# Which rounds the exp of a block's last two VectorE chunks stands in

## The chip, the cores and the metric

The kernel runs on one core of one Trainium2 chip. Its time is the device time of one execution in microseconds (us), the median of three runs. TensorE (PE) multiplies matrices, VectorE (DVE), ScalarE (ACT) and GpSimd (POOL) work on tiles, and SyncE (SP) issues DMAs. Each engine runs its own instructions in the order in which the program holds them; they meet through semaphores.

## What is computed

There are two layers over a graph of N = 3327 nodes with D = 128 features. Layer 0 is an attention whose score is a sum of a row's and a column's number, with a residual and a layer norm. Layer 1 is the long one:

```python
q = (x @ Wq.T).reshape(d, n, h)      # d = 128 maps, n = 3327, h = 8
k = (x @ Wk.T).reshape(d, n, h)
v = (x @ Wv.T).reshape(d, n, h)
a = jnp.einsum('dnh,dmh->dnm', q, k) * d ** -0.5
a = a + adj + adj                    # spatial and edge encoding are both adj
a = jax.nn.softmax(a, axis=2)
out = jnp.einsum('dnm,dmh->dnh', a, v).reshape(n, h * d) @ Wo.T
x = layernorm(x + out)
```

So there are 128 attention maps of 3327 x 3327, each of inner size 8, and every one of their 1.4 billion scores needs an exp.

## The kernel before

**Tiling.** The 128 maps are taken in NG = 32 groups of HG = 4 (variable `g`). The 3327 queries are cut into NBLK = 7 blocks (`b`), six of 476 columns and one of 472 that counts; the 3327 keys into NT = 26 chunks (`i`) of 128 or 127 partitions. A **block** of the program is one pair (g, b): 4 maps x 476 queries against all 26 chunks. There are 32 x 7 = 224 blocks, one after the other, and the engines go from one into the next without a barrier.

**One chunk.** TensorE makes the scores (L154) in two halves of two maps each, 128 x 952 a half, into PSUM tiles `scb`. There are then two ways to exp(2(score + adj)). For the chunks in `times` (i = 0, 3, ..., 24; nine of them) ScalarE takes the exp of a half straight out of PSUM (L1136) and GpSimd multiplies it by exp(2 adj) (L1137). For the other 17, the **VectorE chunks**, VectorE adds adj to the scores of a half and writes the sum `e4` to SBUF (L1139), and ScalarE takes the exp there, in place (L968, in `exp_late`). At last TensorE multiplies each chunk's `e4` by the values and sums over the chunks in `av` (L938, in `products`), which VectorE copies out once a block (L948).

**Rounds.** The order is written out by hand (`rounds`, L917 to L927). The chunks stand in stretches of three, (0, 1, 2), (3, 4, 5), ..., (21, 22, 23), and a last one of two, (24, 25). A stretch (i, i+1, i+2) has three rounds: [(i, 1), (i+1, 0)], [(i, 0), (i+1, 1)], [(i+2, 0), (i+2, 1)], where (i, h) is half h of chunk i. The last stretch has the first two alone. So a block has NR = 26 rounds, called R0 to R25 here, each with two halves; R24 is [(24, 1), (25, 0)] and R25 is [(24, 0), (25, 1)]. R0 of the next block follows R25.

In a round the program issues, in this order: the scores of its two halves (four matmuls, L1125); a few units of side work on TensorE (`work_tensor`); for each half the direct exp and multiply, or the add; then `exp_late(now)`, that is, the exps that earlier rounds have put down in the list `late` for this round; the products of the chunk that stands LAG = 4 rounds back in `order`; and side work on VectorE and GpSimd (`work`). Side work is layer 0 of later rows and the output of earlier ones. Function `lane` gives it room for one VectorE unit in every third round from R4, and in R0, R24 and R25; for one TensorE unit in R3, in every third round from R4, and in R24 and R25.

**The list `late`** (L1142 to L1150) says in which round a VectorE chunk's exp is issued. Its general rule is the last branch: the whole chunk, 128 x 1904, one round after its second half was added. Two chunks of a block have a branch of their own, because 26 % 3 is 2. Chunk 25 (`NT - 1`) has its exp in two halves, each two rounds after its add, so they stand in R0 and R1 of the next block. Chunk 23 (`NT - 3`), whose two adds are both in R23, has its exp in two halves, in R24 and in R25.

**Buffers.** `scb` of the `times` chunks has one PSUM buffer (pool `pe`), so the scores of the next direct exp are computed only after the one before has been read; those of the VectorE chunks have two (pool `pd`). `e4` has seven.

## Time and profile before

| | |
|---|---|
| median of 3 runs (lowest to highest) | 10004.5 us (10001.76 to 10006.51) |
| profiled execution: time, span | 10004.91 us, 10003.1 us |
| ACT busy | 9892.4 us, 99% of the span |
| PE busy | 9461.4 us, 95% |
| DVE busy | 9334.1 us, 93% |
| POOL busy | 9201.7 us, 92% |
| granted TensorE clock | 0.996 |
| L968 ACT exp in SBUF | 4256 instructions, 7104.0 us |
| L1136 ACT exp out of PSUM | 4032 instructions, 4078.6 us |
| L1139 DVE add | 7616 instructions, 8420.0 us |

Read it so: busy time is the time that lies under an engine's instructions, and ScalarE's and VectorE's instructions overlap their neighbours a little, so the sum of the durations (7104.0 + 4078.6 us for ScalarE) is more than the busy time, and even more than the span. In a run of back-to-back instructions what one of them takes is the distance from the end of the one before to its own end, not its duration. The page's 40 slices show the same shares from the second to the last but one: the 224 blocks are alike.

The timeline shows instructions of one engine by start (us from the span's start), duration and line; equal neighbours are merged (x2, x3), and what the engine waited for stands in brackets.

### The profile page before, as it was taken

What the parts mean: (1) busy time and instruction counts of PE and PEld (TensorE: products, weight loads), DVE (VectorE), ACT (ScalarE), POOL (GpSimd) and SP (SyncE); (2) the same over time, 40 slices, a digit from 0 to 9 for tenths busy, and PEclk for the clock granted to TensorE, in tenths of its full rate; (3) what the DMA queues carried; (4) which work ended last, traced back from release to release, by engine and by line L of the source; (5) the groups of instructions that cost most, each with busy time, mean ns of one, the idle gap of its engine ahead of it and who ended that gap; (6) DMA issues with size and microseconds to landing.
All of it is one profiled execution on the core that took longest, in us unless ns stands there. A gap on an engine that the chain in (4) does not pass through costs nothing.

```text
span 10003.1 us, 212173 instructions
## 1 busy us (share of the span) xinstructions
PE 9461.4 (95%) x81923; PEld 3078.5 (31%) x81923; DVE 9334.1 (93%) x11592; ACT 9892.4 (99%) x8352; POOL 9201.7 (92%) x4416
## 2 busy tenths in 40 slices
PE   7999999999999999999999999999999999999998
PEld 2233333333233333323333332333332333332222
DVE  7999999999999999999999999999999999999998
ACT  7999999999999999999999999999999999999998
POOL 7999999999999999999999999999999999999998
PEclk9999999999999999999999999999999999999999
DMA  7665666655656656656566665566665566656554
GB/s 200 200 176 169 177 172 177 178 167 174 177 165 175 182 161 178 177 169 176 165 173 174 181 179 164 163 178 179 177 174 168 164 179 177 175 161 171 167 168 125
DMA packets 1383200, 1728.31 MB, mean 173 GB/s; under 512 B 347463, under 2 KB 1370657, under 8 KB 1378079
## 3 DMA queue, kind: packets, MB, share of 16 engines
q1 hardware_dynamic: 1371828, 1712.03, 60.1%
q8 instruction: 644, 10.55, 0.4%
q10 hardware_dynamic: 10347, 2.61, 0.1%
q14 instruction: 381, 3.12, 0.1%
HBM read 1610.23 MB, written 103.93 MB: 171 GB/s over the span
## 4 chain that ended last, share of the span: by engine, by line
ACT 40%; PE 24%; POOL 16%; issue 11%; DVE 6%; DMA 2%; SPq 1%; POOLq 0%; ACTq 0%; DVEq 0%
ACT e L968 25%; POOL e L1137 16%; ACT e L1136 15%; PE scb L154 12%; PE av L938 11%; DVE e L1139 4%; PE bank L243 1%; DVE o L948 1%; DVE lo L408 0%; DMA q4b<-qT 0%; POOL w L319 0%; DMA at<-ftd 0%; DVE hi L405 0%; DMA k4b<-kT 0%; DVE w L310 0%
## 5 line engine op out<-in xcount | busy, mean ns | idle before, releaser
L1137 POOL TENSOR_TENSOR e<-e,at 128x952 f32<-128x952 f32 (+1 forms) x4032 | 8956.7, 2237 | 718.9 <-ACT e L1136 641.7
L1139 DVE TENSOR_TENSOR e<-scb,at 128x952 f32<-128x952 f32 (+1 forms) x7616 | 8420.0, 1143 | 579.3 <-PE scb L154 477.8
L968 ACT ACTIVATE e<-e 128x1904 f32<-128x1904 f32 (+2 forms) x4256 | 7104.0, 1678 | 2.0 <-DVE e L1139 1.6
L938 PE MATMUL av<-e,v4b 128*32 128x476 f32 x46592 | 5917.6, 572 | 60.6 <-DVE o L948 41.9
L154 PE MATMUL scb<-q4b,k4b 32*128 32x476 f32 (+1 forms) x23296 | 3749.2, 486 | 442.8 <-ACT e L1136 370.8
L1136 ACT ACTIVATE e<-scb 128x952 f32<-128x952 f32 (+1 forms) x4032 | 4078.6, 1012 | 57.5 <-PE scb L154 33.8
L154 PEld LDWEIGHTS scb<-q4b,k4b 32*128 32x128 f32 (+1 forms) x23296 | 1764.2, 189 | 5371.8 <-ACT e L1136 3489.9
L938 PEld LDWEIGHTS av<-e,v4b 128*32 128x32 f32 x46592 | 1059.2, 108 | 1140.0 <-issue 933.0
L243 PE MATMUL bank<-hsb,w 128*32 128x129 f32 (+1 forms) x5200 | 277.8, 285 | 0.0
L328 DVE TENSOR_SCALAR_CACHE_REDUCE dump<-a 128x384 bf16<-128x384 f32 (+2 forms) x468 | 247.1, 528 | 0.6
L319 POOL TENSOR_TENSOR w<-w,a 128x384 f32<-128x384 f32 (+3 forms) x225 | 207.7, 923 | 0.1
L310 DVE TENSOR_SCALAR w<-trow,er 128x129 f32<-128x129 f32 x650 | 201.1, 338 | 0.0
L948 DVE COPY o<-av 128x476 f32<-128x476 f32 (+1 forms) x224 | 145.9, 651 | 8.1 <-PE av L938 7.2
L243 PEld LDWEIGHTS bank<-hsb,w 128*32 128x32 f32 (+1 forms) x5200 | 102.4, 108 | 148.0 <-issue 148.0
L408 DVE SCALAR_TENSOR_TENSOR lo<-bank,hi 128x128 fp32r<-128x128 f32 (+1 forms) x400 | 116.5, 291 | 13.8
L405 DVE TENSOR_SCALAR hi<-bank 128x128 fp32r<-128x128 f32 (+1 forms) x400 | 112.0, 280 | 0.0
L243 PE MATMUL bank<-wv,x1T 128*32 128x128 f32 x1600 | 85.6, 286 | 3.9 <-DVE vb L429 3.9
L243 PE MATMUL bank<-wq,x1T 128*32 128x128 f32 x1600 | 85.4, 285 | 0.0
L243 PE MATMUL bank<-wk,x1T 128*32 128x128 f32 x1600 | 85.4, 285 | 0.0
L243 PE MATMUL bank<-wo,ot 128*32 128x128 f32 x1600 | 85.2, 285 | 0.0
L429 DVE COPY vb<-bank 128x128 f32<-128x128 f32 (+1 forms) x200 | 56.1, 281 | 5.8 <-PE bank L243 5.8
L503 PE MATMUL bank<-ident,o 128*128 128x128 f32 x225 | 52.0, 304 | 0.0
(123 smaller groups left out, 659.7 us busy)
## 6 DMA issues: line engine op xcount, KB each, us to landing
at<-in_adjT_dram SPq DMA_DIRECT2D x1536, 476.0 KB
at<-ftd SPq DMA_DIRECT2D x1674, 238.0 KB
at<-in_adjT_dram SPq DMA_DIRECT2D x256, 472.0 KB
at<-ftd SPq DMA_DIRECT2D x279, 236.0 KB
k4b<-kT SPq DMA_DIRECT2D x128, 415.9 KB
q4b<-qT SPq DMA_DIRECT2D x1528, 29.8 KB
at<-in_adjT_dram SPq DMA_DIRECT2D x186, 208.2 KB
a<-in_adjT_dram SPq DMA_DIRECT2D x50, 504.0 KB
```

What stands on the lines that cost most here:

```text
L154: nc.tensor.matmul(dst, k4[32 * j : 32 * j + H4, first_key(i) : first_key(i) + 2 * r - 1 : 2], q4[32 * j : 32 * j + H4, :nb], start=True, ...
L243: nc.tensor.matmul(dst[c0:c1], w[:, c0:c1], mov, **kw)
L310: nc.vector.tensor_scalar(w, s["t"][:, :, :T3], e, None, op0=ALU.max)
L319: nc.gpsimd.tensor_tensor(w, w, s["a"][n][:, c0 - i0 : c1 - i0, :r], op=ALU.mult)
L328: nc.vector.tensor_scalar(z, a, float(k), None, op0=ALU.is_equal, op1=ALU.add, accum_out=even[:, t, at : at + 1])
L408: nc.vector.scalar_tensor_tensor(lo[:r, o : o + QW], s["b"][:r, :QW], scale, hi[:r, o : o + QW].bitcast(F32), op0=ALU.mult, op1=ALU.subtract,)
L938: nc.tensor.matmul(s.av[32 * j : 32 * j + 32, : s.w], s.v4[:r, j, i * H1 : i * H1 + 32], e[:r, j, : s.w], start=(s.left == NT - 1), stop=( ...
L948: nc.vector.tensor_copy(o4[:, :w], s.av[:, :w])
L968: nc.scalar.activation(e, e, AF.Exp, scale=2.0)
L1136: nc.scalar.activation(eh, z[:r, :, :w], AF.Exp, scale=2.0)
L1137: nc.gpsimd.tensor_tensor(eh, eh, ah, op=ALU.mult)
L1139: nc.vector.tensor_tensor(eh, z[:r, :, :w], ah, op=ALU.add)
```

## The change

```diff
                             if i in times:
                                 continue
                             if NT % 3 == 2 and i == NT - 1:
-                                late.append((now + 2, s, i, 2 * h, 2 * h + 2))
-                            elif NT % 3 == 2 and i == NT - 3:
-                                late.append((now + 1 + h, s, i, 2 * h, 2 * h + 2))
+                                late.append((now + 1, s, i, 2 * h, 2 * h + 2))
                             elif added[i] == 2 and (now + 1, s, i, 0, HG) not in late:
                                 late.append((now + 1, s, i, 0, HG))
```

Chunk 25 keeps its exp in two halves, but each is issued one round after its add: half 0 in R25, half 1 in R0 of the next block. Chunk 23 falls under the general rule: one whole exp, in R24. Nothing else is edited. ScalarE's order from R24 on, with D for a direct exp, h for a late half and W for a whole, and the chunk in brackets:

| round | before | after |
|---|---|---|
| R24 | D(24) h(23) | D(24) W(23) |
| R25 | D(24) h(23) | D(24) h(25) |
| R0 | D(0) h(25) | D(0) h(25) |
| R1 | D(0) h(25) | D(0) |
| R2 | W(1) | W(1) |
| R3 | D(3) W(2) | D(3) W(2) |

The order on TensorE, VectorE, GpSimd and the DMA queues is unchanged.

## The prediction

> **What bounds the kernel now.** I read the busy shares first, then what ScalarE waits for, then one passage from a block to the next, engine by engine. The first line of the page:

> ```profile
> PE 9461.4 (95%) x81923; PEld 3078.5 (31%) x81923; DVE 9334.1 (93%) x11592; ACT 9892.4 (99%) x8352; POOL 9201.7 (92%) x4416
> ```

> ScalarE is full, and what it lacks of the span lies mostly ahead of its first exp at 66 us. The view of the line of the late exps says what it waits for there:

> ```profile
> its engine sat idle before it (us, times) until:
>   DVE e L1139: 1.6, 4
> ```

> 4256 late exps lost 1.6 us in all to VectorE's adds. So today the adds are always early enough; how early decides this case. Now the passage from one block to the next, ScalarE's timeline from R24 on:

> ```profile
> 5075.51 1.06 ACT L968 ACTIVATE e<-e 128x952 f32<-128x952 f32 x1
> 5076.40 1.02 ACT L1136 ACTIVATE e<-scb 128x952 f32<-128x952 f32 x1
> 5077.24 1.07 ACT L968 ACTIVATE e<-e 128x952 f32<-128x952 f32 x1
> 5078.13 1.03 ACT L1136 ACTIVATE e<-scb 128x952 f32<-128x952 f32 x1
> 5078.99 1.05 ACT L968 ACTIVATE e<-e 127x952 f32<-127x952 f32 x1
> 5079.88 1.02 ACT L1136 ACTIVATE e<-scb 128x952 f32<-128x952 f32 x1
> 5080.72 2.74 ACT L968 ACTIVATE e<-e 127x952 f32<-127x952 f32 x2
> 5083.36 0.96 ACT L1136 ACTIVATE e<-scb 128x952 f32<-128x952 f32 x1
> 5084.22 1.78 ACT L968 ACTIVATE e<-e 128x1904 f32<-128x1904 f32 x1
> ```

> These are h(23), D25 (the direct exp of R25), h(23), D0 (that of R0), h(25), D1, then h(25) and W(1) merged, D3, W(2). The ends stand at 5076.57, 5077.42, 5078.31, 5079.16, 5080.04, 5080.90, 5083.46, 5084.32, 5086.00: no gap anywhere. From end to end a late half takes 0.89, a direct half 0.85, a whole 1.68; read the same way in 190 blocks, the medians are 0.886, 0.854 and 1.680. As a check, 15 wholes, 4 late halves and 18 direct ones make 44.12 us, and the median block takes 44.11. So ScalarE's ends are the clock of the kernel.

> **What the change removes.** One late exp a block: chunk 23's two halves become one whole. End to end that is 2 x 0.886 - 1.680 = **0.092 us**, x 224 blocks = 20.6 us. The mean durations say something else:

> ```profile
> L968 ACT ACTIVATE e<-e 128x1904 f32<-128x1904 f32 x2880 | 5299.5, 1840 | 1.0 <-DVE e L1139 0.9
> ...
> L968 ACT ACTIVATE e<-e 128x952 f32<-128x952 f32 x384 | 425.0, 1107 | 0.0
> ```

> 2 x 1.107 - 1.840 = 0.374 us would be 84 us, but neighbours overlap, so a duration is not what an instruction takes. [...]

> **What it moves.** Each of four exps comes at least a round or half a round earlier.
> - W(23) in R24 needs both adds of R23. Its slot is that of the h(23) at 5075.51; the second add ends at 5075.05 in this block. Over 222 blocks the add ends 0.40 us ahead of the slot (median; 0.33 in the tenth percentile). The smallest distance from an add's end to the whole exp that needs it is 0.093 us, met over a dozen times in the trace, so I take 0.09 for the handover. Nothing is lost here; in the few blocks below that it costs under 0.1.
> - The halves of 25 keep about 2 us to their adds. Nothing.
> - D25 comes 0.79 us later behind D24 (a whole between them for a half). D25, h, D0, h, D1 then follow each other as before, and so do TensorE and VectorE, whose scores for R0 and R1 wait for D25 and D0 to read the one `scb` buffer: they only idle 0.8 us more in R25.
> - **W(1) now follows D1 at once**; the h(25) that stood between is gone. W(1) needs the add of (1, 1), and this is the point of the case.

> VectorE's and TensorE's timelines of the same passage (in TensorE's, L154 are scores, L938 products):

> ```profile
> 5079.79 1.15 DVE L1139 TENSOR_TENSOR e<-scb,at 128x952 f32<-128x952 f32 x1
> 5081.18 3.36 DVE L1139 TENSOR_TENSOR e<-scb,at 128x952 f32<-128x952 f32 x3 [0.24 <-PE scb L154]
> 5084.48 0.65 DVE L948 COPY o<-av 128x476 f32<-128x476 f32 x1
> 5085.05 1.14 DVE L1139 TENSOR_TENSOR e<-scb,at 128x952 f32<-128x952 f32 x1
> 5086.11 0.54 DVE L328 TENSOR_SCALAR_CACHE_REDUCE dump<-a 128x384 bf16<-128x384 f32 x1
> ...
> 5086.73 2.21 DVE L1139 TENSOR_TENSOR e<-scb,at 128x952 f32<-128x952 f32 x2
> ```

> ```profile
> 5079.21 0.50 PE L154 MATMUL scb<-q4b,k4b 32*128 32x476 f32 x4 [0.21 <-ACT e L1136]
> ...
> 5081.41 1.42 PE L938 MATMUL av<-e,v4b 127*32 127x476 f32 x8
> ```

> The chain: D0 ends 5079.16, scores 5079.21 to 5079.71, add (1, 1) 5079.79 to 5080.94. It hangs on D0 alone and can't be earlier. **First wait:** W(1) can start at 5080.94 + 0.09 = 5081.03 and, with the 1.78 of an exp that had to wait, ends 5082.81; back to back it would end 1.68 after D1, at 5082.58. Lost: 0.23. In R0 a side unit stands between VectorE's two adds; where it is long, the wait is longer. Block by block in the trace the mean is **0.27**.

> **Then VectorE runs behind.** It does (2, 0), (2, 1), (4, 0), copy, (4, 1), a side unit, (5, 0), (5, 1) nearly without a gap, and ScalarE now comes 0.89 - 0.23 = 0.66 earlier to each. In this block: W(2) needs 5083.39 + 0.09, its slot is 5083.56: nothing. W(4) needs (4, 1), whose end stays between 5086.09 and 5086.19 (0.1 of (4, 0)'s place was TensorE's products of chunk 25, 1.42 instead of 1.00 because they waited for h(25); that wait goes). W(4) then ends at 5087.96 to 5088.06 instead of 5087.87: 0.09 to 0.19 lost. W(5) needs (5, 1), today 5087.79 to 5088.94; it may come up to 0.2 earlier, since ahead of (5, 0) VectorE waited for scores that waited for D3, and D3 is earlier now. Lost: 0.13 to 0.22 here, nothing where R4's side unit is short. From R6 on VectorE's slack of a stretch exceeds what is left.

> The sum over a block is bounded from both sides. If VectorE kept today's distance to D0 throughout, the largest shortfall is 0.65 us (mean of 222 blocks). With every gap after (2, 0) taken out it is 0.37. I take **0.45**: 0.27 + 0.09 + about 0.09, nearer the lower end, because TensorE's two waits do go. 223 passages x 0.45 = 100.4 us.

> **Sum.** 10003.1 - 20.6 + 100.4 = 10082.9 us of span; the profiled execution's time is 1.8 over its span: 10084.7. The median of the runs is 0.4 below the profiled time: **10084**.

> Costed at nothing: GpSimd's multiplies (2.24 each) of the four direct exps R24 to R1, which now come 2.53, 1.74, 1.74 apart instead of thrice 1.74. The products that need the last of them stand in R5, over 3 us later; if that cover went, the products would wait as they do in 79 places today, 38 us in all. DMAs and side work keep their places.

> **Rivals.**
> - *Only the first wait*: VectorE catches up in R2 to R4, the rest of the slack suffices. For it: 0.24 of idle ahead of (2, 0). Against: that idle is TensorE's and stays. 223 x 0.27 - 20.6 = +40: 10044. Chance 0.16.
> - *No catching up*: VectorE's gaps stay though D3 is early. 223 x 0.65 - 20.6 = +124: 10129, or more if the lag reaches the next stretches. Chance 0.16.
> - *Hidden (the other side)*: the add of (1, 1) comes early enough because VectorE and TensorE had 0.8 us more ahead of R0, and the whole exp's 20.6 us remain: 9984. It decides where the loss a block falls under 0.092, that is, where the add ends 0.14 earlier behind D0 than it does. Against it: the scores start 0.05 after D0's end, so time won before D0 isn't passed on. Chance 0.06.
> - *Balance*: a loss of 0 to 0.18 a block, around 10010. Chance 0.08.
> - The forecast, 10050 to 10120: 0.54.

> **Range and chances.** 10032 (the first wait at its least, 0.22: 49 - 21 = +28) to 10135. About 0.2% (20 us) is what a measurement of this kernel tells from no change: faster 0.06, same 0.09, slower 0.85.

> **What would show it.** L968 has 4032 instructions, its 128x952 form gone. The idle time ahead of L968 put down to VectorE's add goes from 1.6 us to about 50 to 100. W(1) starts 0.09 after the add of (1, 1) in nearly every block, and W(4), W(5) in many. VectorE idles 0.8 longer ahead of the add of (1, 0). Wrong if W(1) starts back to back behind D1, if the add of (1, 1) ends less than 2.7 us after D0's start (today 2.81 in the median), or if the lost time lies at a direct exp (a score that is late) rather than at a late one.

## The result and the profile after

The changed kernel takes **10121.3 us** (median of 4 runs, 10116.48 to 10122.84) beside 10003.13 us (9998.15 to 10006.51) of the kernel before in the same session: ratio **1.0117**, 95% interval 1.0105 to 1.013. The forecast was 10084, range 10032 to 10135: right side, inside the range, 37 us short.

The first line of the page of the profiled execution (span 10118.8 us):

```profile
PE 9385.6 (93%) x81923; PEld 3053.3 (30%) x81923; DVE 9293.8 (92%) x11592; ACT 9933.1 (98%) x8128; POOL 9210.5 (91%) x4416
```

224 instructions fewer on ScalarE (8352 to 8128), and every engine's share is lower: all of them wait more. The same passage from a block to the next as in the prediction, first ScalarE: D0, h(25), D1, W(1), D3, W(2):

```profile
5135.37 1.03 ACT L1136 ACTIVATE e<-scb 128x952 f32<-128x952 f32 x1
5136.23 1.06 ACT L968 ACTIVATE e<-e 127x952 f32<-127x952 f32 x1
5137.12 1.02 ACT L1136 ACTIVATE e<-scb 128x952 f32<-128x952 f32 x1
5138.27 1.79 ACT L968 ACTIVATE e<-e 128x1904 f32<-128x1904 f32 x1
5140.18 0.97 ACT L1136 ACTIVATE e<-scb 128x952 f32<-128x952 f32 x1
5141.04 1.78 ACT L968 ACTIVATE e<-e 128x1904 f32<-128x1904 f32 x1
```

Read the ends again: D1 5138.14, W(1) 5140.06, D3 5141.15, W(2) 5142.82. The steps are 1.92, 1.09, 1.67, where back to back they are 1.68, 0.85, 1.68. So 0.24 are lost at W(1) and another 0.24 at D3. Over 190 blocks of full width the median steps are 1.927, 1.079 and 1.679, and 0.904 at D6 instead of 0.854: lost 0.25, 0.23, 0 and 0.05, together 0.53.

VectorE and TensorE in that passage:

```profile
5135.44 1.15 DVE L1139 TENSOR_TENSOR e<-scb,at 128x952 f32<-128x952 f32 x1 [1.06 <-ACT e L1136]
...
5137.03 1.15 DVE L1139 TENSOR_TENSOR e<-scb,at 128x952 f32<-128x952 f32 x1
5138.42 3.26 DVE L1139 TENSOR_TENSOR e<-scb,at 128x952 f32<-128x952 f32 x3 [0.24 <-PE scb L154]
5141.60 0.64 DVE L948 COPY o<-av 128x476 f32<-128x476 f32 x1
```

```profile
5134.71 0.60 PE L154 MATMUL scb<-q4b,k4b 32*128 32x476 f32 x4 [0.88 <-ACT e L1136]
...
5138.65 1.01 PE L938 MATMUL av<-e,v4b 127*32 127x476 f32 x8
5139.59 0.53 PE L154 MATMUL scb<-q4b,k4b 32*128 32x476 f32 x4
...
5142.30 1.00 PE L938 MATMUL av<-e,v4b 128*32 128x476 f32 x8 [0.24 <-DVE o L948]
```

Three readings. The add of (1, 1) ends at 5138.18 and W(1) starts at 5138.27, the handover of 0.09. D3 starts at 5140.18, 0.06 after its scores (5139.59 to 5140.12), which stand in TensorE's queue behind the products of chunk 25. And TensorE idles 0.88, VectorE 1.06 us in R25, for D25: that idling is new.

The waits listed for the late exps' line:

```profile
its engine sat idle before it (us, times) until:
  DVE e L1139: 13.6, 45
```

Only 13.6 us (1.6 before; the prediction named 50 to 100 as a sign), though the wait at W(1) costs a quarter of a microsecond in each of 223 passages. The view counts the gap between a recorded end and the next start. Back to back the next exp starts some 0.18 before the end of the one ahead, and a wait first eats that overlap: of the 0.24 lost at W(1) above, 0.13 is left as a gap. The 45 gaps that are listed are all over 0.15 us, so most of the 223 are not among them. Here only end-to-end steps show what a wait costs.

### The profile page after: what moved, and what is told of

It is laid out like the page before. It is cut to its first block, busy times and chain, and to the rows that moved or that the text cites. A ratio compares the mean times of both kernels' runs of the same rounds, so it can differ in the third digit from the quotient of the medians.

```text
span 10118.8 us, 212173 instructions
## 1 busy us (share of the span) xinstructions
PE 9385.6 (93%) x81923; PEld 3053.3 (30%) x81923; DVE 9293.8 (92%) x11592; ACT 9933.1 (98%) x8128; POOL 9210.5 (91%) x4416
## 4 chain that ended last, share of the span: by engine, by line
ACT 43%; PE 19%; POOL 16%; issue 11%; DVE 8%; DMA 3%; SPq 1%; ACTq 0%; POOLq 0%; DVEq 0%
ACT e L968 30%; POOL e L1137 16%; ACT e L1136 13%; PE scb L154 9%; PE av L938 9%; DVE e L1139 6%; DVE o L948 1%; DMA at<-in_adjT_dram 1%; DMA k4b<-kT 1%; DMA q4b<-qT 1%; DVE lo L408 0%; DVE hi L405 0%; DVE w L310 0%; PE bank L243 0%; SPq L734 0%
## 5 line engine op out<-in xcount | busy, mean ns | idle before, releaser
L1139 DVE TENSOR_TENSOR e<-scb,at 128x952 f32<-128x952 f32 (+1 forms) x7616 | 8385.7, 1143 | 736.2 <-PE scb L154 486.5
L968 ACT ACTIVATE e<-e 128x1904 f32<-128x1904 f32 (+3 forms) x4032 | 7019.0, 1741 | 38.2 <-DVE e L1139 13.6
L938 PE MATMUL av<-e,v4b 128*32 128x476 f32 x46592 | 5852.5, 574 | 112.1 <-DVE o L948 93.1
L154 PE MATMUL scb<-q4b,k4b 32*128 32x476 f32 (+1 forms) x23296 | 3752.8, 487 | 580.9 <-ACT e L1136 531.2
L1136 ACT ACTIVATE e<-scb 128x952 f32<-128x952 f32 (+1 forms) x4032 | 4030.9, 1000 | 94.8 <-PE scb L154 40.5
L154 PEld LDWEIGHTS scb<-q4b,k4b 32*128 32x128 f32 (+1 forms) x23296 | 1767.2, 189 | 5509.3 <-ACT e L1136 3462.1
L938 PEld LDWEIGHTS av<-e,v4b 128*32 128x32 f32 x46592 | 1031.6, 108 | 1141.5 <-issue 880.7
L328 DVE TENSOR_SCALAR_CACHE_REDUCE dump<-a 128x384 bf16<-128x384 f32 (+2 forms) x468 | 247.3, 528 | 0.6
L948 DVE COPY o<-av 128x476 f32<-128x476 f32 (+1 forms) x224 | 144.1, 644 | 5.5 <-PE av L938 5.5
```

The lines of the kernel that those rows point to most:

```text
L154: nc.tensor.matmul(dst, k4[32 * j : 32 * j + H4, first_key(i) : first_key(i) + 2 * r - 1 : 2], q4[32 * j : 32 * j + H4, :nb], start=True, ...
L328: nc.vector.tensor_scalar(z, a, float(k), None, op0=ALU.is_equal, op1=ALU.add, accum_out=even[:, t, at : at + 1])
L938: nc.tensor.matmul(s.av[32 * j : 32 * j + 32, : s.w], s.v4[:r, j, i * H1 : i * H1 + 32], e[:r, j, : s.w], start=(s.left == NT - 1), stop=( ...
L948: nc.vector.tensor_copy(o4[:, :w], s.av[:, :w])
L968: nc.scalar.activation(e, e, AF.Exp, scale=2.0)
L1136: nc.scalar.activation(eh, z[:r, :, :w], AF.Exp, scale=2.0)
```

## The experiments

Theory A, as it stood after this comparison: ScalarE lost 0.53 us a block by waits that begin at D0, less 0.09 for the instruction saved. The rival, B in most runs: another part of the change, or another engine, is to blame. All ratios are against the kernel before, run on the same chip. "D0 to D6" is the distance between the starts of the direct exps of R0 and R6, the median over the trace's full-width blocks; it is 10.29 us in the kernel before and 9.93 in the changed one, where ScalarE back to back would need 9.40.

**Chunk 23's whole exp alone** (chunk 25 as before):

```diff
-                            elif NT % 3 == 2 and i == NT - 3:
-                                late.append((now + 1 + h, s, i, 2 * h, 2 * h + 2))
```

> Chunk 23's whole exp alone; chunk 25 keeps its halves two rounds after their adds. ScalarE: D24 W(23) D25, D0 h(25) D1 h(25) W(1): nothing stands between D25 and D0. Theory A (a direct exp behind another waits for its scores, because the one scb buffer is read by the first; a late exp between them hides that): D0 starts about 0.62 us after D25's end (0.05 to the scores, 0.5 for the four matmuls, 0.06 on), where it would start 0.17 before it; with 0.96 of a direct exp that had to wait its end comes 0.72 late. No wait at W(1) or D3, since h(25) is back between D1 and W(1). 0.72 - 0.09 = 0.63 a block, x 223 = +140: about 10143. Theory B (the loss of the changed kernel belongs to chunk 25's move alone, and the whole exp is free): 20 us faster than before, 9983.

Measured: 10171.88 us, ratio 1.0163 (1.0148 to 1.0179). D25 and D0 in one block, then TensorE's scores of R0 between them:

```profile
5159.11 1.02 ACT L1136 ACTIVATE e<-scb 128x952 f32<-128x952 f32 x1
5160.84 0.96 ACT L1136 ACTIVATE e<-scb 128x952 f32<-128x952 f32 x1 [0.70 <-PE scb L154]
```

```profile
5160.18 0.59 PE L154 MATMUL scb<-q4b,k4b 32*128 32x476 f32 x4 [0.89 <-ACT e L1136]
```

Two direct exps in a row cost 0.82 us (end to end 1.67 instead of 0.85): more than my 0.72, since the four matmuls took 0.59 where I had taken 0.5. Theory B falls: the whole exp isn't free where it leaves a direct exp without a late one behind it. TensorE idles for D25 as long as in the changed kernel (0.89 and 0.88 us), but behind D0 nothing is lost here: the median steps at W(1) and D3 are 1.681 and 0.853, and D0 to D6 is 10.22.

**Chunk 25's halves early, alone** (chunk 23 in halves as before):

```diff
-                                late.append((now + 2, s, i, 2 * h, 2 * h + 2))
+                                late.append((now + 1, s, i, 2 * h, 2 * h + 2))
```

> Chunk 25's halves one round after their adds, as in the changed kernel; chunk 23 keeps its two halves. ScalarE: D24 h(23) D25 h(23) h(25) D0 h(25) D1 W(1). Theory A (the loss comes from W(1) following D1 at once): the waits of the changed kernel at W(1) (0.28 a block) and at D3 (0.27) are there in full, and the 20.6 us of the removed half are not won: the changed kernel's 10121 plus 21, about 10140. Theory B (the loss comes from the whole exp of 23, which puts D25 0.79 later and the three direct exps D25, D0, D1 close together): no loss, about 10004.

Measured: 10167.12 us, 1.0156 (1.0141 to 1.0172). The waits are the changed kernel's: steps of 1.926 and 1.081 at W(1) and D3, D0 to D6 9.96, the median block 44.62 us. (44.62 - 44.11) x 223 = 114 us of the 161, so theory B (no loss) falls. The other 47 us I had not expected. In 41 blocks, each 1.1 to 1.3 us longer (one 1.5), TensorE's granted clock drops. Stretches of the trace (start and end, length, busy time and instructions of PE, its weight loads, DVE, ACT and POOL, then the granted clock, DMA share and GB/s):

```profile
852.00:856.00 4.00, 2.60 (x24) 0.67 (x19) 3.27 (x7) 4.00 (x6) 4.00 (x3) 1.00 0.59 183
856.00:860.00 4.00, 4.00 (x24) 0.65 (x20) 2.37 (x3) 3.28 (x3) 4.00 (x3) 0.57 0.58 186
860.00:864.00 4.00, 3.55 (x40) 1.24 (x36) 3.96 (x6) 3.31 (x3) 3.44 (x2) 1.00 0.04 9
```

A stretch in which TensorE is busy 2.60 of 4 us is followed by one at a clock of 0.57, that is, 3.4 us at 0.50. One matmul of the products takes 1.00 us in such stretches of this run and 0.56 outside them (medians), which is why the blocks that hold one are longer. Past the first 730 us and ahead of the last blocks there is no such drop in the kernel before, and there are 14 in the changed one. The blocks that hold them are 14 us longer in sum, 12% of its loss. Each part of the change alone costs more than the two together (166 and 161 us against 118).

**The other way round**: chunk 23 in halves as before, chunk 25's exp whole by the general rule:

```diff
-                            if NT % 3 == 2 and i == NT - 1:
-                                late.append((now + 2, s, i, 2 * h, 2 * h + 2))
-                            elif NT % 3 == 2 and i == NT - 3:
+                            if NT % 3 == 2 and i == NT - 3:
                                 late.append((now + 1 + h, s, i, 2 * h, 2 * h + 2))
```

> The other way round: chunk 23 in two halves as before, chunk 25's exp whole, one round after its second add (R0). ScalarE: D24 h(23) D25 h(23) D0 W(25) D1 W(1) D3 W(2): as many instructions as in the changed kernel, and again one late exp behind each direct one. Theory A (only the distance from D0 to W(1) and D3 matters): from D0's start to W(1) there are 0.86 + 1.68 + 0.85 = 3.39 us; the add of (1, 1) ends 2.81 after D0's start, so no wait, and D3's scores, ready 3.8 us after D0's start plus 1.03 of D0, meet a D3 at 5.07. The 0.092 a block is won: 20 us faster than before, about 9983. Theory B (VectorE has no slack around the block's end, so that any exp taken out there is lost again in waits): within 10 us of before.

Measured: **9982.91 us**, 0.9978 (0.9969 to 0.9988): faster than both kernels, with the changed kernel's number of instructions. D0, W(25), D1, W(1), D3:

```profile
5065.39 1.03 ACT L1136 ACTIVATE e<-scb 128x952 f32<-128x952 f32 x1
5066.25 1.84 ACT L968 ACTIVATE e<-e 127x1904 f32<-127x1904 f32 x1
5067.93 1.01 ACT L1136 ACTIVATE e<-scb 128x952 f32<-128x952 f32 x1
5068.77 1.85 ACT L968 ACTIVATE e<-e 128x1904 f32<-128x1904 f32 x1
5070.46 1.02 ACT L1136 ACTIVATE e<-scb 128x952 f32<-128x952 f32 x1
```

The ends, 5068.09, 5068.94, 5070.62, 5071.48 from W(25) on, are 0.85, 1.68, 0.86 apart: no wait. The median block takes 44.00 us (44.11 before), D0 to D6 is 10.11, over the 9.93 that the other engines need. So the 0.092 us of the saved instruction are real, and it is the place of the whole exp that decides: between D0 and D1 it gives the others 0.8 us behind D0; between D24 and D25 it takes them away, and ScalarE's own 9.40 is under the 9.93.

**The changed kernel without the products of chunk 25:**

```diff
-                for j in range(HG):
+                for j in range(HG if i < NT - 1 else 0):
                     nc.tensor.matmul(
```

> The changed kernel without the products of chunk 25 (eight matmuls, about 0.95 us of TensorE in R2, between the scores of R2 and those of R3); that part of the sum over keys is left out of the output. Theory A (D3's wait of 0.27 is TensorE's queue: the scores of R3 stand behind those products): D3's wait goes; the wait at W(1) stays at 0.28; with D3 in time, W(4) and W(5) meet VectorE's adds and lose some 0.1 to 0.2 together, as the prediction had it. 10121 - 60 + 20 to 45: 10080 to 10105. Theory B (all of the loss is VectorE's lag, and D3's wait only one place where it shows): no change, 10121.

Measured: 10155.89 us, 1.0142 (1.0126 to 1.0157), *slower* than the changed kernel. From W(1) on: W(1), D3, W(2), D4, W(4), D6:

```profile
5152.67 1.79 ACT L968 ACTIVATE e<-e 128x1904 f32<-128x1904 f32 x1
5154.36 0.95 ACT L1136 ACTIVATE e<-scb 128x952 f32<-128x952 f32 x1
5155.21 1.78 ACT L968 ACTIVATE e<-e 128x1904 f32<-128x1904 f32 x1
5156.89 0.95 ACT L1136 ACTIVATE e<-scb 128x952 f32<-128x952 f32 x1
5157.79 1.79 ACT L968 ACTIVATE e<-e 128x1904 f32<-128x1904 f32 x1
5159.69 0.97 ACT L1136 ACTIVATE e<-scb 128x952 f32<-128x952 f32 x1
```

And VectorE's copy of `av`, with the first products of the new block, which wait for it:

```profile
5156.00 0.64 DVE L948 COPY o<-av 128x476 f32<-128x476 f32 x1
```

```profile
5156.69 1.01 PE L938 MATMUL av<-e,v4b 128*32 128x476 f32 x8 [0.24 <-DVE o L948]
```

D3's wait is gone, its end 0.85 behind W(1)'s. But W(4) and D6 now wait, and D0 to D6 is 9.93 to the hundredth; the median block, 44.54, is the changed kernel's. So D3's wait was one place where a longer delay showed, as theory B had it. The time is worse, and 24 blocks hold half-clock stretches, 14 of them of 10.2 us: the full-width ones among those blocks are 50 us longer in sum, where the changed kernel's 14 cost 14.

**VectorE's scores first.** The changed kernel, with the scores of (1, 0) and (1, 1) issued ahead of those of the direct exps in R0 and R1:

```diff
                         for i, h in rnd:
                             sc.append((pe if i in times else pd).tile([P, 2, 512], F32, name="scb"))
+                        for (i, h), z in sorted(zip(rnd, sc), key=lambda p: n < 2 and p[0][0] in times):
                             for t in range(2):
-                                pair_scores(sc[-1][: kr[i], t, :w], s.k4, s.q4, i, kr[i], 2 * h + t, w)
+                                pair_scores(z[: kr[i], t, :w], s.k4, s.q4, i, kr[i], 2 * h + t, w)
```

> The changed kernel, but in R0 and R1 TensorE gets the scores of the VectorE chunk's half, (1, 0) and (1, 1), ahead of those of the direct exp's half; nothing else moves. Theory A (the waits at W(1), D3 and D6 are all one chain: VectorE's adds of chunk 1 hang on D25 and D0 only because their scores stand in TensorE's queue behind scores that wait for the one scb buffer): add (1, 0) no longer waits for D25, VectorE's idle 1.06 us in R0 goes, add (1, 1) ends some 0.6 to 1 us earlier, and with it all the waits: 10003 - 21 + 0 to 20 = 9982 to 10005. Theory B (VectorE and TensorE are too slow for this stretch in themselves, wherever their scores stand): no gain beyond the first wait, 10060 to 10121.

Measured: 10105.56 us, 1.0102 (1.0086 to 1.0117). W(1) no longer waits (its step is 1.680), but D3, W(2), W(4) and D6 lose 0.11, 0.04, 0.14 and 0.23: D0 to D6 is 9.92. My theory A of one chain through the add of (1, 1) falls, and the time lies in theory B's range: D0 to D6 stays the same, wherever those scores stand.

**Both paths shortened.** The changed kernel without the products of chunk 25 and with VectorE's copy of `av` cut from 476 to 32 columns (643 to 182 ns); and the short copy alone:

```diff
-                    nc.vector.tensor_copy(o4[:, :w], s.av[:, :w])
+                    nc.vector.tensor_copy(o4[:, :32], s.av[:, :32])
...
-                                oT[...], o4[32 * j : 32 * j + H1, c0:w]
+                                oT[...], wq[32 * j : 32 * j + H1, c0:w]
```

> The changed kernel without the products of chunk 25, and with VectorE's copy of av (L948) cut from 476 columns to 32; what it left out is replaced in the output by rows of a weight. Theory A (two paths from D0 to the direct exp of R6, D6, take the same 9.93 us: one through TensorE's queue with the products of chunk 25, one through VectorE's adds and its copy of av, which the first products of the block wait for; ScalarE alone would need 9.40): only with both shortened the time falls. The wait at W(1) stays, 0.28: D0 to D6 9.68 in the median block, whose period falls from 44.53 to about 44.3. Theory B (the distance is set by something else, GpSimd's multiplies for instance): 9.93 and 44.53 as before. The time itself depends on how many blocks run at half clock: 10060 to 10110 under A, 10120 to 10160 under B.

> The changed kernel with the copy of av cut to 32 columns alone (the output as in the run before). Theory A: the path through TensorE still sets D3, whose start stays 4.81 us behind D0's, and nothing but the 0.05 at D6 goes: D0 to D6 9.88, median block 44.48, 10105 to 10121. Theory B (VectorE's path alone sets the distance): D0 to D6 about 9.7, median block 44.3, 10070.

Measured: 10065.03 us, 1.0063 (1.0046 to 1.008), with D0 to D6 9.65 and a median block of 44.26 us; the copy alone 10098.01, 1.0096 (1.0079 to 1.0113), with 9.88 and 44.47. D4, W(4) and D6 with both:

```profile
5110.60 0.95 ACT L1136 ACTIVATE e<-scb 128x952 f32<-128x952 f32 x1
5111.44 1.79 ACT L968 ACTIVATE e<-e 128x1904 f32<-128x1904 f32 x1
5113.12 0.96 ACT L1136 ACTIVATE e<-scb 128x952 f32<-128x952 f32 x1
```

The line of the short copy (count, busy us, mean ns, idle before it):

```profile
L948 DVE COPY o<-av 128x32 f32<-128x32 f32 x224 | 40.7, 182 | 9.9 <-PE av L938 9.9
```

D4, W(4) and D6 are back to back (1.68 and 0.85), and so are those of D3 and W(2), 0.85 and 1.68 in the median block: only W(1)'s own wait is left, as expected to 0.03 us. The products alone gave nothing, the copy alone 0.05, both together 0.28. That is the mark of two paths of nearly the same length: TensorE's queue (scores, products of R1 and R2, scores of R3) to D3, and VectorE's adds and copy, the first products of the new block, which wait for the copy because `av` has one buffer, and the scores after them, to D6.

**Work for TensorE in the idle stretch.** Small matmuls into unused columns, in the kernel with chunk 25 early alone (four, in R0) and in the changed kernel (six, in R25; this edit is shown):

```diff
+                        if n == NR - 1:
+                            i = rnd[1][0]
+                            for t in range(6):
+                                pair_scores(sc[1][: kr[i], t % 2, w : w + 32], s.k4, s.q4, i, kr[i], t % 2, 32)
```

> The kernel with chunk 25's halves early and chunk 23's kept (10167 us), with four more matmuls of 32 columns in R0 behind the products, into columns of scb that nobody reads: they only give TensorE something to do where it idled 1.1 us. Theory A (41 blocks of that run took 1.1 to 1.3 us longer because the granted clock went to 0.50 for 3.4 us behind that idle time): the clock stays at 1.00, those blocks take 44.6 us like the rest, about 10117. Theory B (the long blocks have another cause and the clock only goes with it): no change, 10167, or a little more for the added work.

> The changed kernel with six matmuls of 32 columns more in R25 behind the products, into columns of scb that nobody reads, where TensorE waits 0.7 to 1.1 us for D25. Theory A (14 blocks of the profiled execution lose about 1.1 us each to a granted clock of 0.50): 10121 - 16 = 10105, no block at 0.50 past the first 700 us. Theory B: 10121 or a little more.

Measured: 10162.81 us, 1.0158 (1.0142 to 1.0174), with 39 half-clock stretches (41 without the filler), and 10116.12, 1.0112 (1.0097 to 1.0128), with 9 (14 without). The filler hardly helped, though it did break up the idle gap: in the 3.41 us (the length of the shortest drops) ahead of each of those 39 drops TensorE's longest gap was 0.35 to 0.58 us, where it was 0.96 to 1.10 without the filler. So theory A, one idle gap of 1.1 us as the trigger, falls; B isn't shown, as the time didn't part from the clock. What starts these stretches stays open.

**VectorE's scores first in the faster order**, in every round that has both:

> The faster order (chunk 23 in two halves, chunk 25 whole), with the VectorE chunk's scores ahead of the direct exp's in every round that has both. Theory A (ScalarE is back to back there, 44.00 us in the median block, against 44.02 for 16 wholes, 2 halves and 18 direct exps): nothing to win but the rare long blocks, within 15 us of 9983. Theory B (adds that come later than they could still cost something in that order): 20 us or more below 9983. A direct exp's scores come later by a pair of matmuls, which may cost: slower than 9983 is possible under both.

Measured: 10016.68 us, 1.0013 (1.0004 to 1.0022): 34 us slower than the same order without it. D6's step rises from 0.853 to 0.950 in the median block, which is 0.11 longer in all: 24 of the 34 us. The direct exp pays there for scores that come a pair of matmuls later; nothing is won elsewhere. Theory B falls, and A's bound is missed by 19 us, on the side that the expectation had left open under both.

## Why the prediction was right, and where its sum was short

- **The saved half: 0.092 us a block.** Right: the order with chunk 25 whole has it and nothing else, 23 us faster by the medians (20.6 forecast), median block 0.11 shorter.
- **The first wait, at W(1).** Right in place and cause: 0.28 in the mean, forecast 0.27, and 0.24 in the block shown, forecast 0.23. W(1) starts within 0.12 of the end of the add of (1, 1) in 221 of 223 passages.
- **"D25, h, D0, h, D1 then follow each other as before ... they only idle 0.8 us more in R25."** That is what happened, and the idling by itself costs nothing behind D0: the run with chunk 23 whole alone has it too, and no wait at W(1) or D3. The loss comes from the h(25) that is gone from between D1 and W(1), as the prediction said. But it counted the loss add by add and had no term for the stretch as a whole: ScalarE's own time from D0 to D6 fell from 10.29 to 9.40 us, and TensorE and VectorE need 9.93.
- **W(4) and W(5), 0.18 together.** Mis-sized and misplaced: nothing is lost at them in the changed kernel. The loss is at D3 (0.23) and D6 (0.05), at direct exps, which the prediction had named as a sign against it. The step that failed is "ahead of (5, 0) VectorE waited for scores that waited for D3, and D3 is earlier now": D3's own scores were late, so that D3 starts 4.81 us behind D0 instead of 5.23, 0.42 earlier where the prediction took 0.66; and the first products wait for the copy. In sum 0.53 instead of 0.45, between the bounds of 0.37 and 0.65.
- **Not in the sum: half-clock stretches**, 14 us.
- **How near it came.** 10121 lies 1 us over the band of 10050 to 10120 that had the chance of 0.54, and nearer the rival "No catching up" (10129) than the forecast. That is in part chance: the half-clock stretches were in neither. By the loss in a block, 0.53 stands between the forecast's 0.45 and that rival's 0.65.
- The account: the median passage 44.54 - 44.11 = 0.43 (0.53 - 0.09, within rounding), x 223 = 96; half clock 14; together 110 of the 115.7 us between the spans. The rest is not put down to anything here.
- GpSimd's multiplies, costed at nothing: with TensorE's and VectorE's paths shortened, all waits but W(1)'s went, so GpSimd set none of them in the median block.

## What to carry to other kernels

Where an engine is full, as ScalarE here (98 to 99% of the span), each of its instructions also gives time to the engines that prepare what comes a few instructions later. Moving a long one ahead of a point where those engines must stop and wait takes that time from them behind it (0.8 us in this case). Here the same instruction count was 1.2% slower or 0.2% faster by the place of one whole exp. Where removing one suspected delay only moves the wait downstream, measure the distance between two fixed points; if it stays to the hundredth, look for a second path of the same length, and shorten both.
